# Two graph layers over 16 batches on one core: a value group moved behind the query graph, batch 1's keys by seven products, and one fold moved behind the next unit's scores

## The chip, the cores and the metric

The kernel runs on one core of a Trainium2 chip. The metric is the device time of one execution in microseconds. TensorE is PE in the profile, VectorE is DVE, ScalarE is ACT, GpSimd is POOL, and SP is the engine whose queue issues almost all DMA transfers.

## The reference, cut to what matters

`x` has 16 batches of 1024 nodes with 256 channels, all float32; `adj` is 1024 x 1024. Layer 0 builds queries from a graph that depends on the batch, keys and values from a projection, and attends with four heads of 64 channels:

```python
c_adj = mean(x, channels)                       # one number per node
A_s   = likeness of c_adj of two nodes          # 1024 x 1024, symmetric
g     = relu((x^T @ (adj * A_s)) * para)        # queries, 256 x 1024
k, v  = x @ kv_w                                # keys and values, 1024 x 256 each
out   = softmax(q k^T * scale) v                # four heads
x     = layernorm(x + out)
```

Layer 1 is two graph convolutions (`relu(x @ w_loop + adj @ (x @ w_neigh) + b)`, 256 to 128 channels and back), `(x + h) * 0.5`, a sum with x, and a layernorm.

## The kernel before, in words

**Order.** Everything is unrolled in Python over the 16 batches, and the order on each engine is the order in which `run()` writes the instructions (`manual_schedule`). The batches overlap: while batch b attends, the graph of b+1 is weighed and the convolutions of earlier batches are computed in the gaps.

**Attention** (`Attention`) goes in four units: two pairs of heads times two halves of the query nodes. `scores(u)` makes eight score tiles on TensorE (L594, psum tag `big`, three buffers), exponentials on ScalarE into eight probability tiles (L597), and sums these on VectorE into `acc` (L601, L603), which is then transposed (L605) and reduced to `den_part` (L607). `outputs(u)` multiplies by the values (L614) and transposes the result to `o` on VectorE (L618). `add(u)` folds `den_part` over partitions by a small product on TensorE (L626, tile `den_ps`), and VectorE then inverts it, scales `o` and adds it to the residual `xB` (L630 to L635).

**Queries.** `Queries` (batches 0 and 1) does eight steps of four products each (L473); `end()` multiplies by `para` on VectorE (L479) and takes a relu on ScalarE (L480). From batch 2 on `FastQueries` computes the same by seven block products (L546), with sums of halves on GpSimd (tile `S`, L505 to L508) and VectorE (tile `T`), and an `end()` of sums on VectorE (tiles `P` and `U`, L555 to L563).

**Keys and values.** For batches 0 and 1 `keys` makes eight products of 128x128 by 128x512 (L350) and copies the sums on ScalarE (L352), and `values` makes four groups of four products (`value_group`, L360), each copied out (L362): on VectorE for batch 0, on ScalarE for batch 1. From batch 2 on `KeysValues` does both. `sums()` makes four differences of quarters of `xT` on VectorE (L384 to L387), `load()` fetches sums of the key weights that `sum_key_weights` wrote to DRAM at the start, and `run(between, later)` makes seven products of 512 columns (L405) with the four value groups between them, snapshots on ScalarE, two sums on VectorE (L418, L426), one on GpSimd (L427) and a last copy on ScalarE (L429).

**Between batches 0 and 1** (the branch `more and not c1`) the query steps of batch 1 alternate with the end of batch 0's attention and its layernorm (`BlockedNorm`): `mean`, `squares`, `sum_squares`, `variance` (a fold on TensorE, L324 on VectorE and a power on GpSimd, L326), `scale` (two multiplications on VectorE, L331) and `spread` (two transposes into `x1T` on VectorE, L219, and eight stores on SP, L339). `turn_adj` transposes the rest of the adjacency on VectorE, ten halves of tiles (L956). After scores and outputs of unit 0 of batch 1, `gap0` takes the means of batch 2's x (L260), runs `c1.inner()` of the convolution (L712, which reads `x1T`) and `att.add(0)`.

**Buffers.** Adjacency rows, weighings, probabilities, sums and snapshots share one pool of row tiles (`row_tile`, 25 buffers of 128 x 1024); an instruction that writes into a reused buffer waits for the last readers of what was there.

**The gaps.** In batch 1 `c1` is there and `c2` is not (`both` is None). `between` holds `gap0`, `gap1`, `gap2`, run after the outputs of units 0, 1 and 2; `gap2` ends with `att.add(2)`. Units 0 to 2 add in their gaps, unit 3 in a query step. Batches 0 and 15 have no gaps, and add unit u-1 after the scores of unit u.

## Time and profile before

| | |
|---|---|
| median of 3 runs | 2170.1 us (2170.02 to 2170.28) |
| the profiled execution | 2170.13 us |
| its span | 2168.3 us |
| TensorE busy | 2153.5 us (99%) |
| VectorE busy | 1892.3 us (87%) |
| ScalarE busy | 1027.7 us (47%) |
| GpSimd busy | 367.2 us (17%) |
| batch 0's scores begin | 51.40 us |
| batch 1's scores begin | 151.14 us |
| batch 2's scores begin | 267.99 us |

Times in the profile count from the start of the span. A line of the timeline is: start, length, engine, line of the kernel, operation, what it writes and reads with shapes, how many, and in brackets how long the engine had been idle and what ended that. A line of the waits is: who waited for whom, total us, how often, the longest. TensorE takes each float32 product as two records.

### The profile page before, as it was taken

Reading aid. Unit: us, or ns where it says so; the run is one execution under the profiler, and the core shown is the slowest. Engines: PE = TensorE matmul, PEld = TensorE weight load, DVE = VectorE, ACT = ScalarE, POOL = GpSimd, SP = SyncE. Lnnn points to the kernel's source line nnn. Section 1 sums busy time; section 2 is a strip of 40 time slices with the busy share of each in tenths; the row PEclk is TensorE's granted clock in tenths of the full one; section 3 lists DMA queues with packets and bytes.
Section 4 is the critical chain, followed back from the end, with each engine's and each line's share of the span. In section 5 each row is a group of like instructions: output and inputs, shape, how many; then the busy total and the mean of one; then the engine's idle time right before and its main releaser. Section 6 shows DMA issues by size and latency. Waiting matters only on the chain.

```text
span 2168.3 us, 23079 instructions
## 1 busy us (share of the span) xinstructions
PE 2153.5 (99%) x8054; PEld 1024.9 (47%) x8054; DVE 1892.3 (87%) x2343; ACT 1027.7 (47%) x1346; POOL 367.2 (17%) x208
## 2 busy tenths in 40 slices
PE   9999999999999999999999999999999999999997
PEld 5344444444444444444544445454454444544354
DVE  5978998898998989988889888999989899898965
ACT  4744545545355453445444454445553445535411
POOL 1011130211303113030120302203022130211021
PEclk9999999999999999999999999999999999999999
DMA  9493663846557375573655536566384654744342
GB/s 230 117 136 117 139 158 101 143 130 117 147 127 161 102 127 154 128 171 89 115 165 124 160 88 116 171 122 156 97 123 154 122 155 115 131 137 83 117 138 97
DMA packets 611771, 286.22 MB, mean 132 GB/s; under 512 B 504768, under 2 KB 569152, under 8 KB 611648
## 3 DMA queue, kind: packets, MB, share of 16 engines
q1 hardware_dynamic: 611376, 284.15, 55.5%
q8 instruction: 65, 1.06, 0.2%
q14 instruction: 58, 0.48, 0.1%
q10 hardware_dynamic: 272, 0.52, 0.1%
HBM read 238.16 MB, written 46.46 MB: 131 GB/s over the span
## 4 chain that ended last, share of the span: by engine, by line
PE 97%; DVE 2%; ACT 0%; DMA 0%; issue 0%; SPq 0%; POOLq 0%; DVEq 0%; POOL 0%
PE s L594 20%; PE av L614 20%; PE hu_ps L873 17%; PE g_ps L546 16%; PE v_ps L360 5%; PE k_ps L405 4%; PE t_ps L712 3%; PE h_ps L780 3%; PE hu_ps L719 2%; PE g_ps L473 2%; PE h_ps L781 2%; DVE acc L603 1%; PE h_ps L734 1%; PE u_ps L763 1%; PE k_ps L350 1%; PE den_ps L626 0%
## 5 line engine op out<-in xcount | busy, mean ns | idle before, releaser
L597 ACT ACTIVATE pr<-s 128x1024 f32<-128x1024 f32 x512 | 476.1, 1052 | 176.6 <-PE s L594 176.6
L603 DVE TENSOR_TENSOR acc<-acc,pr 128x1024 f32<-128x1024 f32 x384 | 494.1, 1287 | 41.1 <-DVE acc L603 1.0
L594 PE MATMUL s<-qT,kT 64*128 64x512 f32 x2048 | 457.1, 596 | 0.7 <-ACT qT L480 0.7
L614 PE MATMUL av<-pr,v 128*64 128x512 f32 x2048 | 453.6, 595 | 0.0
L594 PEld LDWEIGHTS s<-qT,kT 64*128 64x128 f32 x2048 | 191.1, 185 | 236.1 <-ACT pr L597 114.1
L614 PEld LDWEIGHTS av<-pr,v 128*64 128x64 f32 x2048 | 141.4, 137 | 300.0 <-issue 285.7
L326 POOL TENSOR_TENSOR rstd<-rstd,neg_half 128x32 f32<-128x32 f32 x16 | 87.1, 5443 | 1111.5 <-DVE rstd L324 1111.5
L459 ACT ACTIVATE wg<-c_row,c_col 128x1024 f32<-128x1024 f32 x128 | 146.9, 1148 | 69.5 <-DVE accB L605 51.3
L465 DVE SCALAR_TENSOR_TENSOR wg<-wg,adj 128x1024 f32<-128x1024 f32 x128 | 149.8, 1209 | 11.3 <-ACT wg L460 10.4
L873 PE MATMUL hu_ps<-adj,R 128*128 128x512 f32 x360 | 158.3, 596 | 0.0
L460 ACT ACTIVATE wg<-wg 128x1024 f32<-128x1024 f32 x128 | 135.3, 1057 | 4.1
L314 ACT ACTIVATE sq<-xB_a 128x1024 f32<-128x1024 f32 x32 | 33.8, 1057 | 194.4 <-DVE xB_a L309 193.1
L360 PE MATMUL v_ps<-kvw_sb,xT 128*128 128x256 f32 x512 | 120.2, 379 | 0.1
L546 PE MATMUL g_ps<-wg,S 128*128 128x512 f32 x224 | 116.7, 603 | 0.0
L360 PEld LDWEIGHTS v_ps<-kvw_sb,xT 128*128 128x128 f32 x512 | 97.2, 190 | 38.4 <-issue 21.0
L546 PE MATMUL g_ps<-T,S 128*128 128x512 f32 x224 | 114.4, 592 | 0.0
L546 PE MATMUL g_ps<-wg,x 128*128 128x512 f32 x224 | 109.0, 599 | 0.0
L873 PE MATMUL hu_ps<-adjT,t 128*128 128x512 f32 x240 | 105.7, 592 | 0.0
L873 PEld LDWEIGHTS hu_ps<-adj,R 128*128 128x128 f32 x360 | 67.3, 190 | 78.9 <-issue 78.4
L601 DVE TENSOR_TENSOR acc<-pr,pr 128x1024 f32<-128x1024 f32 x64 | 76.8, 1200 | 23.7 <-ACT pr L597 23.7
L605 DVE STREAM_TRANSPOSE accB<-acc 128x1024 f32<-128x1024 f32 x64 | 79.7, 1245 | 3.2
L889 ACT COPY snap<-hu_ps 128x512 f32<-128x512 f32 x15 | 8.8, 586 | 150.2 <-PE hu_ps L873 150.2
(185 smaller groups left out, 2916.0 us busy)
## 6 DMA issues: line engine op xcount, KB each, us to landing
adj<-in_adj_dram SPq DMA_DIRECT2D x128, 512.0 KB, 4.5
adj<-adjT SPq DMA_DIRECT2D x120, 512.0 KB, 10.2
para<-in_L_gnn_para_dram SPq DMA_DIRECT2D x32, 512.0 KB, 3.3
xB_a<-in_x_dram SPq DMA_DIRECT2D x128, 128.0 KB, 4.2
x1d<-xB_a SPq DMA_DIRECT2D x128, 128.0 KB, 3.4
x<-x1d SPq DMA_DIRECT2D x16, 1024.0 KB, 15.4
xB<-in_x_dram SPq DMA_DIRECT2D x120, 128.0 KB, 4.5
x<-in_x_dram SPq DMA_DIRECT2D x15, 1024.0 KB, 7.0
```

The costliest lines, as they stand in the source:

```text
L326: nc.gpsimd.tensor_tensor(self.rstd, self.rstd, neg_half, ALU.pow)
L360: nc.tensor.matmul(pv[:, ts(i, C)], xT[:, cc, ts(g * per + i, P)], kvw_sb[:, cc, C:2 * C], start=(cc == 0), stop=(cc == NC - 1))
L405: nc.tensor.matmul(dst, self.a[n], self.w[n], start=not again, stop=True, skip_group_check=again)
L459: nc.scalar.activation(wg, self.c_row, AF.Abs, bias=self.c_col[:, t:t + 1], scale=-1.0)
L460: nc.scalar.activation(wg, wg, AF.Tanh, scale=-0.5)
L465: nc.vector.scalar_tensor_tensor(wg, wg, 1.0, self.adj.pop(t), op0=ALU.add, op1=ALU.mult)
L546: nc.tensor.matmul(self.p[n], x_n[:, k, :], w_n, start=(k == 0), stop=(k == TJ - 1))
L594: nc.tensor.matmul(ps[:, ts(s, FB)], self.kT[rows, pair, ts(mt, P)], self.qT[rows, pair, ts(j, FB)], start=True, stop=True)
L597: nc.scalar.activation(pr, ps, AF.Exp)
L603: nc.vector.tensor_add(acc, acc, pr)
L614: nc.tensor.matmul(pav[s * HD:(s + 1) * HD, :], self.v[:, mt, pair * P + s * HD:pair * P + (s + 1) * HD], self.pr[mt][:, ts(s, FB)], start ...
L873: nc.tensor.matmul(dst, self.x[n][:, k, :], half_adj[w][:, k, :] if w else of_rows(rows, k), start=(start and k == 0), stop=(k == TJ - 1), ...
```

## The change

It has three parts. `values` of batch 0 makes three of its four groups, and the fourth comes after `q.end()`, ahead of the attention. In the transition from batch 0 to batch 1 `KeysValues` takes the place of `keys` and `values`: its sums and its load are written ahead of `norm.variance()`, and its `run` is written after `load_next()` and ahead of `norm.scale()`, `norm.spread()` and `turn_adj`, where `keys` and `values` were written after these. And where a batch has gaps and a convolution `c1` but no `c2`, which is batch 1 alone, `att.add(2)` moves from `gap2` to behind the scores of unit 3.

```diff
-    def values(b, xT, copy=nc.scalar.copy):
+    def values(b, xT, copy=nc.scalar.copy, groups=NT * C // FB):
         v = work.tile([P, NT, C], F32, tag="v", name=f"v_{b}")
-        for g in range(NT * C // FB):
+        for g in range(groups):
             value_group(b, v, xT, g, copy)
         return v
...
-        def run(self, between, later):
+        def run(self, between=lambda: None, later=lambda: None):
...
-        v = values(0, xT, nc.vector.tensor_copy)
+        v = values(0, xT, nc.vector.tensor_copy, 3)
...
         qT = q.end()
+        value_group(0, v, xT, 3, nc.vector.tensor_copy)
...
             def gap2():
                 if both:
                     c2.last()
-                att.add(2)
+                    att.add(2)
...
-                if u and not between:
+                if u and (not between or u == 3 and not both):
                     att.add(u - 1)
...
             if more and not c1:
-                xT = ready["xT"]
+                kv = KeysValues(b + 1, ready["xT"])
...
                 q.step(5)
                 q.step(6)
+                kv.sums()
+                kv.load()
                 norm.variance()
                 xB = load_blocked(b + 1, f"a{b + 1}")
                 q.step(7)
                 qT = q.end()
                 load_next()
+                kT, v = kv.run()
                 norm.scale()
                 norm.spread()
                 turn_adj((2, 3, 5, 6, 7))
-                kT, v = keys(b + 1, xT), values(b + 1, xT)
```

## The prediction

> **What bounds the kernel now.** I read the page first: busy time, then the chain that ended last.

> ```profile
> PE 2153.5 (99%) x8054; PEld 1024.9 (47%) x8054; DVE 1892.3 (87%) x2343; ACT 1027.7 (47%) x1346; POOL 367.2 (17%) x208
> PE 97%; DVE 2%; ACT 0%; DMA 0%; issue 0%; SPq 0%; POOLq 0%; DVEq 0%; POOL 0%
> ```

> TensorE sets the time almost alone, so an edit can win only work taken from its queue or a wait in it. Second, what TensorE waited for:

> ```profile
> PE den_ps L626 <- DVE den_part L607: 1.0, 2, 0.8
> PE s L594 <- ACT qT L480: 0.7, 1, 0.7
> ```

> These are the only two waits of the list that the change touches. By the timeline 0.69 us is at 51.40, where batch 0's scores wait for its queries, and 0.78 at 215.75, the fold of the third unit in batch 1. (The other 0.18 is in batch 2.) Third, the stretch between batches 0 and 1, on TensorE (start, length, instruction):

> ```profile
> 137.28 7.03 PE L350 MATMUL k_ps<-xT,kvw_sb 128*128 128x512 f32 x16
> 144.14 7.07 PE L360 MATMUL v_ps<-kvw_sb,xT 128*128 128x256 f32 x32
> 151.14 7.14 PE L594 MATMUL s<-qT,kT 64*128 64x512 f32 x32
> 165.23 3.84 PE L712 MATMUL t_ps<-w1n_sb,x1T 128*128 128x128 f32 x32
> 168.90 0.31 PE L626 MATMUL den_ps<-den_part,fold 128*128 128x32 f32 x2
> ```

> and on VectorE:

> ```profile
> 139.73 2.36 DVE L331 TENSOR_TENSOR xB_a<-xB_a,rstd 128x1024 f32<-128x1024 f32 x2 [1.02 <-POOL rstd L326]
> 142.00 2.36 DVE L219 STREAM_TRANSPOSE x1T<-xB_a 128x1024 f32<-128x1024 f32 x2
> 144.29 6.01 DVE L956 STREAM_TRANSPOSE adjT<-adjB 128x512 f32<-128x512 f32 x10
> 154.29 1.22 DVE L601 TENSOR_TENSOR acc<-pr,pr 128x1024 f32<-128x1024 f32 x1 [3.99 <-ACT pr L597]
> 155.62 7.87 DVE L603 TENSOR_TENSOR acc<-acc,pr 128x1024 f32<-128x1024 f32 x6
> 164.80 1.22 DVE L607 TENSOR_REDUCE den_part<-accB 128x32 f32<-128x1024 f32 x1
> 169.25 0.52 DVE L630 RECIPROCAL rden<-den_ps 64x16 f32<-64x16 f32 x2 [2.60 <-PE den_ps L626]
> ```

> The reader is to see two margins: VectorE idles 3.99 us before the row sums, and finishes den_part at 166.02, 2.9 us before TensorE's fold wants it at 168.90.

> [...] VectorE takes L331, L219, L956 and L601 above in program order, though L601 is what TensorE waits for in the end. [...] So I use starts: 16 records of keys from 137.28 to 144.14 are 0.429 us each, two records to a product, 0.858 per product. [...] in batch 2, where two GpSimd sums (298.75 to 303.30) fall on the row sums: 9.64 us in place of 7.87 above, 0.89 for each.

> ```profile
> 265.51 0.69 DVE L426 TENSOR_TENSOR kT<-ksnap,k_ps 128x512 f32<-128x512 f32 x1 [1.33 <-PE k_ps L405]
> ...
> 294.74 9.64 DVE L603 TENSOR_TENSOR acc<-acc,pr 128x1024 f32<-128x1024 f32 x6
> ```

> **Part 1, fourth value group of batch 0 behind the query graph.** TensorE's work is the same (4 matmuls, 1.73 us: a quarter of the 6.91 that the chain in order of time gives for four such groups). It now lies between the last query step and the scores, where it covers the latency of the queries: the first product with para starts 1.73 us earlier (47.30), its relu ends at 49.6, the group at 50.7. The 0.69 goes. What is late next is the second relu, which now ends (51.3) before the first exponential is due (51.7); before, it stood in front of it, and that unit's scores took 7.42 in place of 7.14, so 0.28 more goes. Does TensorE starve at the front? Query step 1 moves to 24.8 and needs VectorE's second weighting: behind the third value copy it runs 22.3 to 23.5. Covered by 1.3 us; uncovered each microsecond would cost one. The displaced copy (0.69 on VectorE) lies before the row sums at 53.7, free. **−0.97**, from −1.0 to −0.7.

> **Part 2, keys of batch 1 by seven products.** Eight products become seven: −0.858. The same routine in batch 2 runs from 254.75 to the scores at 267.99: 13.24, less a 0.14 fold inside it, 13.10. Here the old routine took 151.14 − 137.28 = 13.86. **−0.76**, from −0.86 to −0.6.
> The rest it issues: four differences on VectorE (0.65 apart, rows L384 to L387: 2.6 us) go before the variance, into the 2.74 idle ahead of 133.96; if they were late, the deviation would be, and that has 8 us to spare below. The reload of the sums (256 KB) enters SP's queue behind para (122.2 to 123.4) and ahead of the 17 loads of the next batch, which move 0.5 us and are wanted no earlier than 40 us on; wanted itself at 140.7, with the like sizes landing in 3 to 10 us. ScalarE swaps two copies of 1.01 for five of 0.59, GpSimd gets one sum of 1.27, both idle there; were one late, products 4 and 3 would wait one for one. Key snapshot 1 waits for two relus (to 139.8) and ends 140.4, its product is due at 140.7: margin 0.3. The x1d stores (8, 7.6 us of SP) start 9 us later, ahead of the line store wanted at 162; they end near 158.
> Row tiles: five more short-lived ones pass through the ring; I count no more live at once than before. Cost nothing.

> **Part 3, what waits behind the new VectorE sums.** The routine now stands ahead of L331, L219 and L956. Its second VectorE sum needs the product that ends late: in batch 2 it starts 10.76 after the first product, less 0.14: 10.6, so 147.9 here. Queued behind it: itself 0.6, scaling 2.27, x1T 2.29, the ten transposes 6.01 (starts 139.73, 142.00, 144.29, end 150.30). So the row sums start at 159.05 where they started at 154.29; from there to the end of den_part is 166.02 − 154.29 = 11.73, so 170.78. TensorE, 0.76 early, asks at 168.14. New wait in TensorE: 170.83 − 168.14 = **2.69**. Who else waits: t_ps for x1T, done at 153.0, wanted 164.5: hidden. GpSimd's four S sums, which started at 164.54 on tiles freed by the unit's outputs, will also wait for the row sums to release these, so from about 166.9, beside the last row sum: not shown before, so bounded. Below: no collision, 0. Above: two sums, 1.8. A gain is excluded, as it takes nothing away. I take **+0.6**: one collided add, (9.64 − 3×1.31)/3 = 1.9 for 1.31. After it TensorE and VectorE of unit 1 both stand some 2.5 later, and the idle of 1.07 before 203.96 takes what is left over on VectorE.

> **Part 4, third fold behind the fourth unit's scores, batch 1.** The 0.78 wait leaves TensorE. But VectorE shows no gap from 213.20 to 251.85, and what follows is chained to its end: squares on ScalarE, P copy at 252.90, U sums from 253.50; L558 ends at 255.38 and frees the PSUM that key product 2 takes at 255.61. Moving the fold reorders VectorE's work and shortens none. With TensorE 0.8 earlier, product 2 waits instead: only 255.61 − 255.38 − 0.06 = **−0.17** is won. Bounds −0.78 (chain not binding) and +0.8 (VectorE left 0.8 late by further GpSimd collisions in unit 1).

> **Sum:** −0.97 − 0.76 + 2.69 + 0.6 − 0.17 = +1.39. The profiled execution took 2170.13 (span 2168.3, 1.8 around it), the median of the runs is 2170.1: so 2171.5.

> **Rivals.** (a) The backlog is covered, and the fold doesn't wait: −0.97 − 0.76 − 0.17 = −1.9, 2168.2. For: 2.9 us of margin and 3.99 of idle are there now. Against: 147.9 + 11.2 of queue ends after 159 whatever the margin. (b) Slower: GpSimd's S sums start as soon as the means are done (162.3) and all four fall on row sums. Price, L632 in batch 2 under one: 0.69 to 1.75, 1.06 each, 4.24, all in front of den_part: −0.97 − 0.76 + 2.69 + 4.24 − 0.17 = +5.0, 2175.2. It decides from where three or more fall there. Against: the S sums waited for outputs, of tiles that VectorE now reads last. (c) Part 4 pays in full: +0.78, 2170.9.

> **Chances.** Forecast 0.70, (a) 0.12, (b) 0.07, (c) 0.11. The forecast's own range is 2169.9 to 2173.3 (−1.0 − 0.86 + 2.4 − 0.78 and −0.7 − 0.6 + 2.69 + 1.8, with part 4 at 0); to leave out less than 0.2 it reaches down to (a), and up by 0.1 for part 4's loss. A measurement here can tell about 0.2%, 4.3 us: faster than 2165.8 0.02, slower than 2174.4 0.06, within 0.92.

> **What would show it.** Part 1: no wait for qT L480, first scores near 50.7. Part 2: k_ps L405 products in the first transition, 13.1 us to the scores. Part 3: L956 after L426 with the row sums first starting near 158 (all is 1 us early by then), and den_ps L626 waiting some 3 us for den_part L607. Part 4: no wait at the third fold, a new one of about 0.6 before the second L405 of the next transition. I am wrong if den_ps waits under 1 us or over 5, or if batches from 2 on lose their even 133.2 us.

## The result and the profile after

| | before | after |
|---|---|---|
| median of 15 runs each | 2170.34 us (2170.02 to 2171.27) | 2175.45 us (2174.15 to 2176.44) |
| ratio | | 1.0023, interval 1.0016 to 1.003 |
| profiled execution, its span | 2170.13, 2168.3 us | 2174.41, 2172.6 us |

The change makes the kernel 5.1 us slower; the forecast was 2171.5, and its range ended at 2173.4. The profiled execution is one of the cheaper runs of the changed kernel, 1.0 us under its median. The runs spread over 2.3 us, where those of before spread over 1.3.

Busy time and the chain that ended last, on the page of after:

```profile
PE 2154.6 (99%) x8052; PEld 1025.3 (47%) x8052; DVE 1897.3 (87%) x2349; ACT 1028.8 (47%) x1349; POOL 372.4 (17%) x209
PE 94%; DVE 4%; ACT 0%; DMA 0%; issue 0%; SPq 0%; DVEq 0%; POOLq 0%; POOL 0%; ACTq 0%
```

TensorE runs two records fewer, one product, and yet is busy 1.1 us longer. That is the first sign that some products ran slowly. What TensorE waited for in after:

```profile
PE den_ps L626 <- DVE den_part L607: 3.5, 2, 3.3
PE k_ps L405 <- DVE U L556: 0.2, 1, 0.2
```

The wait for `qT` is gone, and so is the 0.8 us of batch 1's third fold. Batch 1's first fold, which did not wait before, now waits 3.3 us, and a key product has a new wait. TensorE's timeline in after, at the front, between batches 0 and 1, and in batch 1:

```profile
50.72 7.14 PE L594 MATMUL s<-qT,kT 64*128 64x512 f32 x32
...
149.32 7.14 PE L594 MATMUL s<-qT,kT 64*128 64x512 f32 x32
156.39 7.09 PE L614 MATMUL av<-pr,v 128*64 128x512 f32 x32
163.40 3.84 PE L712 MATMUL t_ps<-w1n_sb,x1T 128*128 128x128 f32 x32
170.56 0.41 PE L626 MATMUL den_ps<-den_part,fold 128*128 128x32 f32 x2 [3.32 <-DVE den_part L607]
170.90 8.83 PE L594 MATMUL s<-qT,kT 64*128 64x512 f32 x32
```

The last line carries the surprise. The same 32 products take 7.14 us at 149.32 and 8.83 us behind the wait. The table by stretches gives the reason; its columns are the stretch, its length, busy time of PE, PEld, DVE, ACT and POOL with the number of instructions, the granted TensorE clock, DMA share and GB/s:

```profile
171.00:172.00 1.00, 1.00 (x6) 0.53 (x8) 0.95 (x4) 0.00 (x0) 0.54 (x1) 1.00 0.00 0
172.00:173.00 1.00, 1.00 (x6) 0.40 (x4) 0.95 (x2) 0.93 (x1) 0.00 (x0) 0.64 0.00 0
173.00:174.00 1.00, 1.00 (x5) 0.35 (x2) 0.98 (x2) 0.69 (x2) 0.00 (x0) 0.50 0.00 0
174.00:175.00 1.00, 1.00 (x6) 0.49 (x4) 1.00 (x2) 0.43 (x1) 0.00 (x0) 0.50 0.55 197
175.00:176.00 1.00, 1.00 (x6) 0.40 (x4) 1.00 (x2) 0.89 (x1) 0.00 (x0) 0.66 1.06 225
176.00:177.00 1.00, 1.00 (x8) 0.40 (x6) 1.00 (x1) 0.79 (x2) 0.00 (x0) 1.00 0.86 197
```

The clock is at 1.00 when TensorE resumes at 170.56. In this trace's own records it is 1.00 or 0.50 and nothing between, so the means put its fall at 172.28 (0.36 missing, so 0.72 us of the stretch slow) and its return at 175.68: 3.4 us at half speed. What is missing adds up to 0.36 + 0.50 + 0.50 + 0.34 = 1.70 us, and the scores are 8.83 − 7.14 = 1.69 us longer.

**The account by starts on TensorE**, after minus before. First key product of batch 1: 136.31 − 137.28 = −0.97. Scores of batch 1: −1.82. First fold: 170.56 − 168.90 = +1.66; L712 ahead of it still stood at −1.83, so 3.49 lost. Clock +1.69 and the fold itself +0.10, making +3.45. The rest of batch 1 with the third fold: −0.05, so batch 2's L712 stands at 285.47 for 282.07, +3.40. From there the 133.2 us per batch are kept but for 0.27 at 1722, so TensorE's last instruction stands at +3.67. The remaining 0.6 of the span lies behind VectorE's last instruction, in the final store: 2172.6 − 2166.64 = 5.96 us against 2168.3 − 2162.97 = 5.33.

### The profile page after: what moved, and what is told of

It is laid out like the page before. It is cut to its first block, busy times and chain, and to the rows that moved or that the text cites. A ratio compares the mean times of both kernels' runs of the same rounds, so it can differ in the third digit from the quotient of the medians.

```text
span 2172.6 us, 23090 instructions
## 1 busy us (share of the span) xinstructions
PE 2154.6 (99%) x8052; PEld 1025.3 (47%) x8052; DVE 1897.3 (87%) x2349; ACT 1028.8 (47%) x1349; POOL 372.4 (17%) x209
## 3 DMA queue, kind: packets, MB, share of 16 engines
q8 instruction: 65, 1.06, 0.2%
## 4 chain that ended last, share of the span: by engine, by line
PE 94%; DVE 4%; ACT 0%; DMA 0%; issue 0%; SPq 0%; DVEq 0%; POOLq 0%; POOL 0%; ACTq 0%
PE s L594 20%; PE av L614 19%; PE hu_ps L873 17%; PE g_ps L546 15%; PE v_ps L360 5%; PE k_ps L405 4%; PE g_ps L473 3%; PE h_ps L780 3%; PE hu_ps L719 2%; PE t_ps L712 2%; PE h_ps L781 2%; DVE acc L603 1%; PE h_ps L734 1%; PE u_ps L763 1%; PE den_ps L626 0%; DVE wg L465 0%
## 5 line engine op out<-in xcount | busy, mean ns | idle before, releaser
L597 ACT ACTIVATE pr<-s 128x1024 f32<-128x1024 f32 x512 | 476.4, 1051 | 180.8 <-PE s L594 180.8
L603 DVE TENSOR_TENSOR acc<-acc,pr 128x1024 f32<-128x1024 f32 x384 | 495.1, 1289 | 41.1 <-DVE acc L603 1.0
L594 PE MATMUL s<-qT,kT 64*128 64x512 f32 x2048 | 458.5, 597 | 0.0
L594 PEld LDWEIGHTS s<-qT,kT 64*128 64x128 f32 x2048 | 192.2, 186 | 236.0 <-ACT pr L597 110.0
L326 POOL TENSOR_TENSOR rstd<-rstd,neg_half 128x32 f32<-128x32 f32 x16 | 87.1, 5442 | 1113.3 <-DVE rstd L324 1113.3
L360 PE MATMUL v_ps<-kvw_sb,xT 128*128 128x256 f32 x512 | 120.9, 379 | 0.1
L360 PEld LDWEIGHTS v_ps<-kvw_sb,xT 128*128 128x128 f32 x512 | 97.2, 190 | 40.1 <-issue 22.5
L601 DVE TENSOR_TENSOR acc<-pr,pr 128x1024 f32<-128x1024 f32 x64 | 76.8, 1200 | 19.2 <-ACT pr L597 19.2
L607 DVE TENSOR_REDUCE den_part<-accB 128x32 f32<-128x1024 f32 x64 | 78.0, 1219 | 2.2
```

The source lines that it names most:

```text
L326: nc.gpsimd.tensor_tensor(self.rstd, self.rstd, neg_half, ALU.pow)
L360: nc.tensor.matmul(pv[:, ts(i, C)], xT[:, cc, ts(g * per + i, P)], kvw_sb[:, cc, C:2 * C], start=(cc == 0), stop=(cc == NC - 1))
L594: nc.tensor.matmul(ps[:, ts(s, FB)], self.kT[rows, pair, ts(mt, P)], self.qT[rows, pair, ts(j, FB)], start=True, stop=True)
L597: nc.scalar.activation(pr, ps, AF.Exp)
L603: nc.vector.tensor_add(acc, acc, pr)
```

## Experiments

Thirteen kernels. Each is set against runs of the kernel before on the same chip (medians 2170.15 to 2170.29), and all differences below are against these. Where the interval of a ratio takes in 1, as for every difference under 1 us here, the runs alone don't prove it; there the profiles carry the reading.

**Parts alone.** *e1_part1* takes of the diff the value group behind the query graph, and nothing else.

> Only the fourth value group of batch 0 moves behind the query graph. Theory of the prediction: the 0.69 us wait for the queries and the 0.28 us of the slow first scores both go, 0.97 us less than before, so about 2169.4. Rival, that the group leaves a hole at the front where the query steps start 1.7 us earlier: no gain, 2170.3 or more.

Measured 2169.19 (−0.96; ratio 0.9996, 0.9987 to 1.0004); at batch 2 the profile is 1.17 us early, 0.14 of it from the start-up. Part 1 pays as worked out.

*e2_part2* takes the keys by seven products with their order, and nothing else.

> Only the keys of batch 1 by seven products, placed ahead of scaling, spread and transposes. Theory (wait and clock): 0.85 us less of products, a wait of about 3.3 us in the first fold, and behind it a halved TensorE clock that costs 1.7 us as in the profile after or up to some 3 more: 2174.5 to 2177, all of the loss and more than the whole change loses. Rival (the loss is the wait alone): -0.85 + 3.3 = +2.5, 2172.8.

Measured 2176.51 (+6.36; ratio 1.003, 1.0019 to 1.0042), with a den_ps wait of 3.3 us and the clock at 0.50 from 172 to 175. Part 2's place carries the whole loss, and the wait's own length doesn't explain it.

*e3_part3* moves the third fold, and nothing else.

> Only the third fold of batch 1 behind the fourth unit's scores. Theory: VectorE's chain to the next keys holds, and of the 0.78 us at most 0.2 is won: 2170.1 to 2170.3, and a new wait of about 0.6 us ahead of the next keys' second product. Rival: the whole 0.78 is won, 2169.5.

Measured 2170.80 (+0.65; ratio 1.0004, 0.9995 to 1.0012). At batch 2 the profile is 0.01 us from before, and 0.07 late at batch 1's first key product: all but 0.06 of the fold's 0.78 is lost again at the key products of batch 2. Two further slips, of 0.35 and 0.34 us in batches 9 and 11, no theory had.

At batch 2 the three parts alone stand at −1.17, +4.57 and +0.01, which is +3.41 together; the whole change stands at +3.40.

**Is it the clock?** *e4_fill*, *e9_fill12* and *e10_fill4* are the changed kernel with 24, 12 or 4 idle transposes of an identity just ahead of batch 1's first fold, which do no useful work:

```diff
                 c1.inner()
+                if not both:
+                    warm = bank_psum("warm")
+                    for _ in range(24):
+                        nc.tensor.transpose(warm[:, 0:P], ident, ident)
                 att.add(0)
```

> The changed kernel with 24 transposes of the identity, results unused, put into TensorE's queue ahead of the first fold of batch 1: at about 0.12 us each they fill 2.8 of the 3.3 us of waiting. The data wait stays as it is. Theory (clock): TensorE no longer idles long, the clock stays at 1.00 behind the fold, scores of unit 1 take 7.14 in place of 8.83, and the time falls by 1.7 to 3.9 us to about 2171.8, with runs closer together than the 2.3 us of the changed kernel. Rival (the extra comes from contention of GpSimd, VectorE or transfers): no change from 2175.4.

> The changed kernel with 12 identity transposes (instead of the 24 of e4_fill) ahead of batch 1's first fold. The fold comes at the same moment as in e4_fill, since both wait for the same PSUM bank; only TensorE's idle time ahead of it differs: about 2.3 us here, 1.33 us there. If a wait of this length is still free of the clock loss, the median is that of e4_fill (about 2.5 us over the kernel before in one call: 2172.8 to 2173.4) and the granted clock behind the fold stays at 1.00. If the loss starts below 2.3 us, it is 1.7 to 2.8 us more (2174.5 to 2176) with a clock near 0.57 for some 4 us.

> The same with 4 transposes: TensorE's idle time ahead of the fold is about 3.25 us, as long as in the changed kernel, and the fold comes at the same moment as in e4_fill and e9_fill12. Clock theory: 1.7 to 2.8 us over e4_fill, 2175 to 2176.2, with a granted clock near 0.57 for some 4 us behind the fold. Rival (the gain of e4_fill came from the place of the fold or from a shifted order, not from TensorE being busy): the median of e4_fill, 2173.3.

The filler takes a PSUM bank, so that the fold waits for VectorE's `o` (L618) in all three and comes at nearly the same moment, 170.97 to 171.20, later than in after. Only the idle time ahead of it differs:

| idle transposes | TensorE idle in the profile | scores behind it | median (lowest to highest) |
|---|---|---|---|
| 24 | 1.33 us | 7.14 us | 2173.33 (2173.03 to 2173.95) |
| 12 | 2.63 us | 7.14 us | 2174.72 (2173.21 to 2176.7) |
| 4 | 3.50 us | 9.90 us | 2176.14 (2173.86 to 2177.12) |

TensorE's lines in e10_fill4, where the fold itself is slow too:

```profile
171.20 0.63 PE L626 MATMUL den_ps<-den_part,fold 128*128 128x32 f32 x2 [3.50 <-DVE o L618]
171.76 9.90 PE L594 MATMUL s<-qT,kT 64*128 64x512 f32 x32
```

and in e4_fill:

```profile
170.97 0.41 PE L626 MATMUL den_ps<-den_part,fold 128*128 128x32 f32 x2 [1.33 <-DVE o L618]
171.31 7.14 PE L594 MATMUL s<-qT,kT 64*128 64x512 f32 x32
```

With the filler long enough, the changed kernel is 1.9 us faster than without it (each against its own runs of before), although it does more work and its fold comes 0.4 us later, and the runs' spread shrinks from 2.3 to 0.9 us. The rival, that the place of the fold made the gain, falls: with 4 transposes the place is the same and the loss is back. The e4_fill median lies 1.5 us above the expected 2171.8; the later fold explains 0.4 of this, and in the profiles the final store is 0.5 us longer than in after; the rest is open. With 2.63 us of idle time the outcome differs from run to run. The profiled one shows no loss (clock 1.00 throughout):

```profile
171.16 0.41 PE L626 MATMUL den_ps<-den_part,fold 128*128 128x32 f32 x2 [2.63 <-DVE o L618]
171.50 7.14 PE L594 MATMUL s<-qT,kT 64*128 64x512 f32 x32
```

Of all runs six lie at 2173.2 to 2173.8, ten at 2174.3 to 2175.2, one at 2176.7. The means of the second and third group lie 1.3 and 3.1 us above the first, near the 1.7 and 3.4 us that half speed costs over 3.4 or 6.8 us. The granted clock on record for each whole run agrees: 0.998 in all six of the first group, 0.997 in nine of the other eleven (3.4 us at half speed takes 0.0008 off it). In e10_fill4 the means put the half speed from 170.56 to 177.36, 6.8 us, twice as long as in after:

```profile
170.00:171.00 1.00, 0.00 (x0) 0.00 (x0) 1.00 (x2) 0.00 (x0) 1.00 (x2) 0.78 0.00 0
...
174.00:176.00 2.00, 2.00 (x6) 0.68 (x4) 2.00 (x3) 1.32 (x2) 0.00 (x0) 0.50 0.81 209
176.00:178.00 2.00, 2.00 (x8) 0.87 (x6) 1.95 (x2) 1.32 (x2) 0.00 (x0) 0.66 0.89 268
```

The trace also records each change of the clock, and these lie whole steps of 3.413 us apart: in after at 5.02 (the first record), 172.28 (49 steps later) and 175.69 us (one more), in e10_fill4 at 6.71, 170.55 (48) and 177.38 us (two more). In the step that ended with the fall TensorE was idle for 1.70 us in after, 2.85 in e10_fill4 and 3.16 in e2; in the profile of e9_fill12, which kept its clock, no step held more than 1.68 of the gap. The first record comes at 4.4 to 6.9 us, so one and the same gap is divided differently between the steps from run to run. Whether the runs of e9_fill12 differ for this reason was not shown, and a limit can't be read off: at the end of before a step with 1.88 us idle was followed by no fall.

**Is it VectorE's order?** *e5_scale_spread_early* leaves scaling and `x1T` to the key routine, which runs them between its two sums, where VectorE idled 6.82 us; only the ten transposes stay behind it:

```diff
-                kT, v = kv.run()
-                norm.scale()
-                norm.spread()
+                kT, v = kv.run(later=lambda: (norm.scale(), norm.spread()))
```

> The changed kernel with scaling and spread of the norm written inside the key routine, ahead of product 4, where VectorE stood idle 6.82 us. Theory: VectorE's backlog at the row sums shrinks by 4.6 us, more than the wait of 3.3, so the fold doesn't wait and the clock stays: -0.97 - 0.85 - 0.1 against before, 2168.4. Rival (the wait comes from GpSimd's sums or the products themselves): the fold still waits over 1 us and the time stays above 2171.

Measured 2169.45 (−0.84; ratio 0.9997, 0.9988 to 1.0005), 1.05 us above the theory. The den_ps wait of batch 1 is gone:

```profile
167.04 0.31 PE L626 MATMUL den_ps<-den_part,fold 128*128 128x32 f32 x2
```

Batch 2 starts 1.90 us early, which is what rival (a) of the prediction gave. A slip of 0.27 in batch 12 and 1.2 us more in the final store (6.54 us from VectorE's last instruction to the end, 5.33 before) give most of it back in the profiled execution.

*e6_scale_early* runs the scaling alone there (`kv.run(later=norm.scale)`), so that x1T's 2.3 us stay in front of the row sums.

> As the run before but only scaling moves, not the spread: VectorE's backlog shrinks by 2.3 us, so the fold waits about 1.0 us. Theory (the clock falls only behind a long wait): the clock stays at 1.00 and the wait costs its own length, about 1 us over the run with both moved, 2169.4. Rival (any wait of TensorE here costs clock): 1.7 us or more on top, 2171 or more.

Measured 2170.62 (+0.33; ratio 1.0002, 0.9994 to 1.001): the wait is back at 1.0 us, and batch 2 stands 1.29 us later than in e5. The clock stays at 1.00 and the 13 runs lie within 0.6 us. This short wait costs about its length.

**Where does the moved fold's gain go?** *e7_no_part3* is e5 with the third fold back in `gap2`.

> Scaling and spread early, but the third fold of batch 1 back behind the third unit, where it was before. Theory: that move is worth at most 0.2 us, so 2168.4 to 2168.6, with the 0.8 us wait back at the third fold. Rival: 0.78 slower than with the fold moved, 2169.2.

Measured 2169.89 (−0.40; ratio 0.9999, 0.999 to 1.0007): 0.44 over e5, though batch 2 is only 0.14 later; it has two slips where e5 has one. *e8_squares_late* is e5 with batch 1's squares behind ScalarE's copy of `P`, so that VectorE's `U` sums no longer wait for them:

```diff
-                q.step(2, lambda: (norm.mean(), norm.squares()))
+                q.step(2, lambda: (norm.mean(), c2 and norm.squares()))
...
-                qT = q.end(norm.sum_squares)
+                qT = q.end(lambda: (c2 or norm.squares(), norm.sum_squares()))
```

In batch 1 there is no `c2`, so the squares move there alone.

> Scaling and spread early, fold moved, and in batch 1 the squares of the norm written behind the copy of P on ScalarE, so that the sums which free the PSUM of the next keys no longer stand behind them. Theory (the fold's gain is held by the chain mean, squares, copy of P, sums): 0.6 us are won over the run without it, 2167.8, and the next keys don't wait. Rival (something else holds the second key product): no gain.

Measured **2167.30** (−2.99; ratio 0.9987, 0.998 to 0.9993), with batch 2 early by 2.83, another 0.93 over e5. It beats both kernels. ScalarE in after:

```profile
254.27 2.19 ACT L314 ACTIVATE sq<-xB_a 128x1024 f32<-128x1024 f32 x2 [13.09 <-DVE xB_a L309]
256.37 0.57 ACT L555 COPY P<-g_ps 128x512 f32<-128x512 f32 x1
```

and in e8_squares_late, where the copy no longer stands behind 2.1 us of squares and no key product waits:

```profile
247.83 0.58 ACT L555 COPY P<-g_ps 128x512 f32<-128x512 f32 x1 [12.08 <-PE g_ps L546]
248.78 2.19 ACT L314 ACTIVATE sq<-xB_a 128x1024 f32<-128x1024 f32 x2 [0.37 <-DVE xB_a L309]
```

*e11_squares_late_all* does the same in every batch from 1 on.

> e8_squares_late with the squares behind the copy of P in every batch from 1 on, not in batch 1 alone. Theory (the short slips of 0.27 to 0.37 us in later batches and the new wait of batch 1 are one chain, ScalarE's squares ahead of the copy of P): no slip in the profile and a median no higher than that of e8_squares_late, about 2167.3. Rival (in the later batches the squares are needed sooner, so variance and scale get late): above 2168, with a new wait from batch 2 on in every batch.

Measured 2167.41 (−2.78; ratio 0.9987, 0.9981 to 0.9994): no different from e8, with no slip in either profile.

*e12_fold_squares_late* and *e13_fold_squares_late_all* are the kernel before with the fold moved and the squares late, in batch 1 or in all batches.

> The kernel before with the third fold of batch 1 behind the scores of unit 3 (as in e3_part3), and batch 1's squares behind the copy of P. Theory (the wait of the fold was won and given back at the key product that waits for the PSUM bank behind the squares): the 0.78 us of the fold's wait are kept now, about 0.8 us under the kernel before and under e3_part3: 2169.3 to 2169.6, the profile 0.7 to 0.9 us earlier at batch 2. Rival (the place of the fold brings nothing in itself): 2170.2, as the kernel before.

> e12_fold_squares_late with the squares behind the copy of P in every batch from 1 on. Theory (the 0.95 us won at batch 2 are given back where a stop of 0.35 to 0.47 us on VectorE or ScalarE reaches TensorE through the squares ahead of the copy of P, which leaves it 0.2 us of room): no slip in the profile, and a median 0.6 to 1.0 us under the kernel before, 2169.2 to 2169.6. Rival (the gain is lost in another way, for example in the tail): 2170.0 to 2170.3, as e12_fold_squares_late.

e12 gave 2170.25 (+0.06; ratio 1.0001, 0.9993 to 1.0009), a miss: batch 2 is 0.95 us early, but slips of 0.35 and 0.42 in batches 9 and 11 take it back. In batch 9 the slip begins on VectorE (e12):

```profile
1287.47 5.21 DVE L603 TENSOR_TENSOR acc<-acc,pr 128x1024 f32<-128x1024 f32 x4
1293.16 2.56 DVE L603 TENSOR_TENSOR acc<-acc,pr 128x1024 f32<-128x1024 f32 x2 [0.47 <-DVE acc L603]
```

VectorE stops for 0.47 us within its row sums, with no other engine named. VectorE stays some 0.37 late up to the `U` sums, and a key product waits 0.35. e13 has the same stop at the same 1293.16 but no slip, and gave 2169.51 (−0.71; ratio 0.9997, 0.9988 to 1.0005, so the median's gain itself is not certain): its chain keeps 1.5 us of room there (from the end of L558 to the start of the second key product), where before has 0.16 in every batch from 2 on. Each of the other profiles has such a stop of 0.46 to 0.47 in the row sums too, at another place: before has it at 1210.96, where it reached nobody. In after the slip at 1722 begins on ScalarE, with 0.35 us between two squares that run back to back in before.

The places have a pattern in these traces. Number the instructions of VectorE's queue as the trace has them, waits included: in all 15 profiles each of these stops in the row sums comes ahead of an instruction whose number is 64 more than a multiple of 128, the 1728th in before (64 + 13 · 128), the 1856th in e12 and e13. ScalarE's stop in after comes ahead of its 1600th, 64 + 12 · 128. Not every such place shows a stop. By this pattern an edit shifts the stops by the number of instructions that it adds or takes away ahead of them; no run tests that by itself. What makes the engine stop there was not shown.

## Why the prediction was wrong

**Part 1** was right: −0.97 forecast, −0.97 in the profile, −0.96 alone. **Part 2** was right in size: −0.76 forecast, −0.85 in the profile.

**Part 3** was right in its mechanism. The queue of VectorE in after:

```profile
146.84 0.69 DVE L426 TENSOR_TENSOR kT<-ksnap,k_ps 128x512 f32<-128x512 f32 x1 [6.82 <-PE k_ps L405]
147.45 2.35 DVE L331 TENSOR_TENSOR xB_a<-xB_a,rstd 128x1024 f32<-128x1024 f32 x2
149.72 2.36 DVE L219 STREAM_TRANSPOSE x1T<-xB_a 128x1024 f32<-128x1024 f32 x2
152.01 6.01 DVE L956 STREAM_TRANSPOSE adjT<-adjB 128x512 f32<-128x512 f32 x10
157.94 1.18 DVE L601 TENSOR_TENSOR acc<-pr,pr 128x1024 f32<-128x1024 f32 x1
159.22 8.75 DVE L603 TENSOR_TENSOR acc<-acc,pr 128x1024 f32<-128x1024 f32 x6
169.28 1.22 DVE L607 TENSOR_REDUCE den_part<-accB 128x32 f32<-128x1024 f32 x1
```

Every step stands where the sum put it, 0.97 earlier for Part 1: the row sums at 157.94 (159.05 − 0.97 = 158.08), the end of den_part at 170.50 (170.78 − 0.97 + 0.6 = 170.41). The first GpSimd sum starts at 164.57, released by `acc`, and one row sum collides (2.10 us, the other five 1.22): the group takes 8.75 us in place of 7.87, so 0.88 where 0.6 was taken. (The 0.6 spread the excess of batch 2 over three additions; the prediction's own 0.89 for each, from the same lines, was the right figure.) TensorE lost 3.49 us there where 2.69 + 0.6 = 3.29 was forecast. The 6.82 at the head of this list is the idle time that e5 uses.

**The step that failed** is the price of that wait. The prediction wrote the new wait as **2.69** plus **+0.6** and carried it into the sum as if a TensorE that waits loses only the time of the wait. But in after the clock falls to 0.50 behind it, and the next scores take 8.83 us for 7.14. None of the signs that the prediction named for being wrong came: the wait lay between 1 and 5 us, and the later batches kept their 133.2 us. No sign looked at the products just behind the wait. In the profiled execution the account stands 4.28 − 1.39 = 2.89 us over the sum: 1.79 behind the wait (1.69 the clock, 0.10 the fold itself), 0.20 for the wait, 0.12 for Part 4, −0.09 for Part 2, 0.27 for the slip and 0.6 for the final store. In the median the clock costs more, about 2.3 us; this is an estimate from after minus e4_fill, each against its own runs of before (5.11 − 3.18 = 1.93), and the 0.41 us by which e4_fill folds later. The 0.5 us of the final store, if it holds in the median, would make it 2.8.

The profile of before did not show the missing term: on its list of TensorE's waits the longest, once TensorE has started, is 0.78 us. What the runs show of it is the half clock (0.50) for 3.4 us in after and 6.8 in e10_fill4, changes of the clock in steps of 3.413 us, and runs of one kernel that differ. A whole idle step was not needed: in after no step of 3.413 us was idle throughout (the wait of 3.32 us took 1.62 and 1.70 us of two), and yet the clock fell; a wait of 2.63 us (e9_fill12) seems to bring it down in most runs.

**Part 4** was right in its mechanism, with −0.17 forecast: the gain is lost again at the key products of batch 2. The account gives −0.05, the rest of batch 1 included; alone the part won 0.06. It is not only "product 2" that waits: product 1 already does, for L556, ahead of the sum that the prediction watched. In before and in after:

```profile
254.75 1.88 PE L405 MATMUL k_ps<-xT,kvw_sb 128*128 128x512 f32 x4
257.71 2.32 PE L405 MATMUL k_ps<-xT,kvw_sb 128*128 128x512 f32 x4 [0.19 <-DVE U L556]
```

e8 shows the reason by taking it away.

**The rivals.** (a), the covered backlog, is what e5 makes by order: 1.9 us early at batch 2, as it said. (b) gave nearly the measured time, 2175.2, by luck: it took four collisions of 1.06 us, where one row sum is slowed, by 0.88, and the clock makes up the rest. (c) did not come.

## What to carry to other kernels

A new wait of TensorE can cost more than its length: in after the clock fell to 0.50 behind one of 3.32 us, and the scores took 1.69 us longer. Waits of 1.0 and 1.3 us brought no such loss, and one of 2.6 us seems to have brought it in most runs. For a wait that comes out longer than the short ones, price the work behind it at half clock for 3.4 us (after) or 6.8 (e10_fill4), or fill the gap with idle products (e4_fill, 1.9 us faster). When a routine is moved ahead of others on VectorE, which took L426, L331, L219, L956 and L601 in the order written (146.84 to 157.94 in after), look first for the idle time inside it and put the displaced work there: e5 needed one line. And a gain on the bounding engine was kept here only where the chain that feeds it next had room: 0.2 us of room let stops of 0.4 us through in several profiles. Taking the squares out of that chain gave 1.1 us of room in batch 1 (e8) and 1.9 in the later batches too (e11), and the two best times, 2167.30 and 2167.41.
